# Two-layer graph attention on one core: the softmax row sums are folded to 32 partitions by transfers, and the MLP chunks run in another order

## The chip, the cores and the metric

The kernel runs on one core of one Trainium2 chip. The metric is device time in microseconds of one execution. Before the change three runs took 3472.78, 3475.09 and 3479.8 us; their median is 3475.09 us.

## What is computed

There are 16 graphs of 1024 nodes with 256 features, and an integer adjacency matrix of 1024 x 1024 for each. Two layers follow each other, each with a layer norm and a ReLU ahead of it and a residual around it. All arithmetic is float32.

```python
# layer 0, per graph: 8 heads of 32 columns, q = k = v
normed = layer_norm(h, gamma1, beta1)            # h = relu(layernorm(x))
scores = einsum('hqd,hkd->hqk', qkv, qkv) / sqrt(32)
attn   = softmax(where(adj > 0, scores, -inf))
h      = h + einsum('hqk,hkd->hqd', attn, qkv)
y      = layer_norm(h, gamma2, beta2)
x      = x + h + gelu(y @ W1 + b1) @ W2 + b2     # W1 256x1024, W2 1024x256
# layer 1, per graph: one head over all 1024 nodes
f      = relu(layernorm(x))
logits = (f@W@a_1)^T + f@W@a_2 + (f@W) @ a_12 @ (f@W)^T
a      = softmax(where(adj > 0, leaky_relu(logits, 0.2), -9e15))
x      = x + elu(f @ W_1 + (a @ f) @ W_2)
```

What matters here is the denominator of the first softmax: for each query and head, the sum over 1024 keys of the exponentials.

## The kernel before

Scores are kept transposed, with the keys on the 128 partitions and the queries along the free dimension. A **unit** of layer 0 is one block of 128 keys (`kt`, 8 of them), one half of 512 queries (`qh`, 2) and one group of 4 heads (`g`, 2), so a graph has 32 units. Units with the same `qh` and `g` form a **group** of 8. In a unit TensorE (PE) writes the scores of 4 heads (`scores`, line 990), VectorE (DVE) adds the mask out of PSUM (line 1011, two instructions of 128x1024), ScalarE (ACT) takes the exponential in place (line 1014, two instructions), and one unit later PE multiplies the values by them (`weigh`, line 1027).

The denominators are built beside that. The exponentials of `kt` 0 are written into two tiles `acc` of 128x1024 (heads 0, 1 and heads 2, 3). Those of `kt` 1 to 7 land in tiles `e`, of which there are five, and each is added to `acc` by an accumulating transfer that GpSimd (POOL) issues (`add_up`, line 1051). Each such transfer waits until the one before it on the same `acc` has landed, and an `e` tile is free again when its transfer has landed. In graph 0 the odd `kt` are added by DVE instead. After the last `kt` of a group `weigh` copies the weighed values out (`os`, line 1042) and puts the group on a list. Two units later `total` (line 924) sums `acc` over its 128 partitions: PE multiplies it by a column block of ones, four products of 512 columns, one for each head (line 929), and ACT copies the result `den` to SBUF as `ds` (line 937). `invert` (line 942) transposes `ds` by 16 small products with a selection matrix `each_head`, DVE takes the reciprocal, and `finish` transposes `os`, scales it and adds it to `h`.

Layer 0's MLP and the whole of layer 1 of graph b run while PE does the attention of graph b+1. They are a generator `rest` (line 1114), whose order is written out in lines 1341 to 1420: `expand(c)` is W1 for a chunk of 256 rows, `contract(c)` is W2 for it, then come the projections, the logits (`weights`) and the weighed sums (`attend`). Six streams (attention, rest, preparation, prologue of the next graph, masks, set-up) are merged by places in lines 1492 to 1497. A step can also be put off with `defer(us, f)`: it is issued once a running count of estimated microseconds has passed. All this only fixes the order of instructions on each engine and queue; every engine runs its own list in order, and POOL's transfers and SyncE's (SP's) transfers are each issued in list order too.

Before chunk 2 is prepared, `rest` waits (line 1348) until both groups of the second query half are finished. While it waits, attention units follow each other without MLP work between them.

Of the kernel before, what the change touches and what calls it, by code (L numbers as in the profile page):

```python
# [9 lines left out]
F32 = mybir.dt.float32  # L10
# [4 lines left out]
ALU = mybir.AluOpType  # L15

P = 128
# [477 lines left out]
def fast_path(  # L495
# [28 lines left out]
    nc = tc.nc  # L524
# [3 lines left out]
    GH = 4  # L528
# [20 lines left out]
    midp = pool("midp", 3)  # L549
    ep = pool("ep", 5)  # L550
    accp = pool("accp", 2)
    lp1 = pool("lp1", 6)
    tmpp = pool("tmpp", 2)
    smallp = pool("smallp", 3)
# [45 lines left out]

    each_head = const.tile([P, GH], F32, name="each_head")
    nc.vector.tensor_copy(each_head, ident[:, ::HD])
    ident8 = const.tile([P, P], FP8, name="ident8")
    nc.vector.tensor_copy(ident8, ident, saturate=False)
    ones = const.tile([P, HD], F32, name="ones")
# [318 lines left out]
    def total(b, qh, g, os, accs):  # L924

        den = ps_tile([P, QW], f"den_{b}_{g}_{qh}")
        for j in range(GH):
            for acc in accs:
                nc.tensor.matmul(
                    den[j * HD : (j + 1) * HD, :],  # L930
                    ones,
                    acc[j // 2][:, j % 2, :],
                    start=acc is accs[0],
                    stop=acc is accs[-1],
                )
        ds = tmpp.tile([P, QW], F32, tag="w2", bufs=3, name=f"ds_{b}_{g}_{qh}")
        nc.scalar.copy(ds, den)
        totalled.append((b, qh, g, ds, os))

    finished = {}  # L940

    def invert(b, qh, g, ds, os):

        pt = ps_tile([P, TPH, GH], f"ptds_{b}_{g}_{qh}")
        for t in range(TPH):
            for c in range(0, P, HD):
                nc.tensor.matmul(
                    pt[c : c + HD, t, :], ds[:, t * P + c : t * P + c + HD], each_head, start=True, stop=True
                )
        rl = smallp.tile([P, TPH, GH], F32, tag="rl", name=f"rl_{b}_{g}_{qh}")  # L950
        ready = defer(1.0, lambda: nc.vector.reciprocal(rl, pt))
        turns.append((1, lambda: finish(b, qh, g, rl, ready, os)))

    def finish(b, qh, g, rl, ready, os):
        h = hs[b]
        run_deferred(ready)
        finished[b, qh] = finished.get((b, qh), 0) + 1
        clock[0] += 0.5
        pt = ps_tile([P, TPH, P], f"ptos_{b}_{g}_{qh}")
        for t in range(TPH):  # L960
            nc.tensor.transpose(pt[:, t, :], os[:, t * P : (t + 1) * P], ident)
        ot = tmpp.tile([P, TPH, GH, HD], F32, tag="w2", bufs=3, name=f"ot_{b}_{g}_{qh}")
        nc.vector.tensor_mul(
            ot, pt.rearrange("p t (j d) -> p t j d", d=HD), rl.unsqueeze(3).to_broadcast([P, TPH, GH, HD])
        )
        ho = h[qh][:, :, g * P : (g + 1) * P]
        nc.gpsimd.tensor_add(ho, ho, ot.rearrange("p t j d -> p t (j d)"))

    def attention(b, st):
# [52 lines left out]
        def weigh(qh, g, kt, es):  # L1022
            if kt == 0:
                acc[g, qh] = pso.tile([P, QW], F32, tag="o", name=f"o_{b}_{g}_{qh}")
            o = acc[g, qh]
            for j in range(GH):
                nc.tensor.matmul(  # L1027
                    o[j * HD : (j + 1) * HD, :],
                    va[:, kt, (g * GH + j) * HD : (g * GH + j + 1) * HD],
                    es[j // 2][:, j % 2, :],  # L1030
                    start=(kt == 0),
                    stop=(kt == NT - 1),
                )
            if b == 0 and kt % 2:

                if kt > 1:
                    for n, (e, w) in enumerate(zip(es, odds[g, qh])):
                        defer(1.0 + 2.5 * n, lambda e=e, w=w: nc.vector.tensor_add(e, e, w))
                odds[g, qh] = es
            if kt == NT - 1:  # L1040
                c = tmpp.tile([P, QW], F32, tag="w2", bufs=3, name=f"os_{b}_{g}_{qh}")
                nc.vector.tensor_copy(c, o)
                weighed.append((b, qh, g, c, [s[g, qh] for s in (sums, odds) if s]))

        sums, odds = {}, {}


        def add_up(qh, g, kt, e, i):
            if b == 0 and kt % 2:
                return  # L1050
            nc.gpsimd.dma_start(sums[g, qh][i], e, accum_op=ALU.add)  # L1051

# [61 lines left out]
    def rest(b, st, tails):  # L1114
# [4 lines left out]
        def load(c):  # L1119
            for t in range(c * TPC, (c + 1) * TPC):  # L1120
                xt.append(xbp.tile([P, D], F32, tag="xb", name=f"xb_{b}_{t}"))
                nc.sync.dma_start(xt[t], rows(x, b, t))
# [222 lines left out]
        hid = {0: (yield from expand(0))}  # L1345
        ask(turn, 1)
        yield from tails[b]()
        while finished.get((b, 1), 0) < NG:
            yield 0.0, None
        prepare(b, st, 2)  # L1350
        load(2)
        hid[1] = yield from expand(1)
        ask(turn, 2)
        prepare(b, st, 3)
        yield from contract(0, hid[0])
        load(3)
        hid[2] = yield from expand(2)
        ask(turn, 3)
        prepare1(0)
        yield from contract(1, hid[1])  # L1360
        hid[3] = yield from expand(3)
        prepare1(1)
        fT = st["fT"] = midp.tile([P, DC, N], F32, tag="mid", name=f"fT_{b}")
# [201 lines left out]
```

## Time and profile before

| | |
|---|---|
| median of three runs | 3475.09 us |
| the profiled execution, its own time | 3465.53 us |
| its span in the trace | 3463.8 us |
| PE busy | 3421.5 us, 99% |
| DVE busy | 2751.4 us, 79% |
| ACT busy | 1857.5 us, 54% |
| POOL busy | 1416.9 us, 41% |
| accumulating transfers | 864 of 512 KB, 71.5% of the time of 16 DMA engines |
| SP's transfers | 137.56 MB, 15.9% |
| granted TensorE clock | 0.998 |

The span holds 119015 instructions. Each line of a group of instructions gives its source line, the engine, the tile written and the tiles read, the count, the busy time, the mean duration of one in nanoseconds, and the time that the engine sat idle before it with what ended that. A busy share is an average over stages with different limits. TensorE's float32 products are recorded as two passes each, so a product of the program is two records.

### The profile page before, as it was taken

The numbers are of one execution on the slowest core, as the hardware profiler recorded it, in microseconds if no ns is written. First come the engines' busy times: TensorE is split into PE (matmuls) and PEld (weight loads), VectorE is DVE, ScalarE is ACT, GpSimd is POOL, SyncE is SP. The second block draws the span as 40 slices with busy tenths as digits, with TensorE's granted clock in tenths as the row PEclk, the third lists the DMA queues.
The fourth block names the chain that finished last, engine by engine and source line by source line (L and its number), as shares of the span: only waits on it lengthen the run. The fifth ranks groups of instructions, "written<-read, shape, count | busy, mean of one in ns | idle before, by whom it ended". The sixth has DMA issues, their size and how long they took to land. (4 is left out here: it accounts for less than half of the span.)

```text
span 3463.8 us, 119015 instructions
## 1 busy us (share of the span) xinstructions
PE 3421.5 (99%) x52478; PEld 1644.7 (47%) x52478; DVE 2751.4 (79%) x5194; ACT 1857.5 (54%) x2184; POOL 1416.9 (41%) x1708
## 2 busy tenths in 40 slices
PE   7999999999999999999999999999999999999998
PEld 2344444444444444444444444444444444444477
DVE  6888788787878878888887887878878788887754
ACT  5555555555555555555555555555555555555522
POOL 4443443434444344443444434344343443433220
PEclk9999999999999999999999999999999999999999
DMA  8799989999899998999999899998999989899730
GB/s 195 154 183 181 185 164 194 177 193 185 164 185 176 185 187 169 184 171 191 189 177 186 166 189 179 188 187 168 186 178 193 186 163 184 170 193 180 153 64 14
DMA packets 281902, 598.56 MB, mean 173 GB/s; under 512 B 94880, under 2 KB 130080, under 8 KB 281376
## 3 DMA queue, kind: packets, MB, share of 16 engines
q0 software_dynamic: 124416, 453.04, 71.5%
q1 hardware_dynamic: 156672, 137.56, 15.9%
q8 instruction: 414, 6.78, 0.8%
q14 instruction: 112, 0.92, 0.1%
q10 hardware_dynamic: 288, 0.26, 0.0%
HBM read 104.21 MB, written 16.78 MB: 35 GB/s over the span
## 5 line engine op out<-in xcount | busy, mean ns | idle before, releaser
L1014 ACT ACTIVATE e<-e 128x1024 f32<-128x1024 f32 x852 | 895.9, 1057 | 947.6 <-DVE e L1011 715.3
L1051 POOL DMA_DIRECT2D acc<-e x864 | 756.2, 891 | 1447.4 <-DMA acc<-e 664.6
L1011 DVE TENSOR_TENSOR e<-s,mk 128x1024 f32<-128x1024 f32 x852 | 1004.0, 1218 | 180.1 <-PE s L990 148.4
L990 PE MATMUL s<-kT 32*64 32x512 f32 x8192 | 577.3, 615 | 2.9 <-DVE odd L1011 2.9
L1027 PE MATMUL o<-e,va 128*32 128x512 f32 x3456 | 462.9, 606 | 2.1 <-ACT e L1014 2.1
L571 PE MATMUL pa<-gw,e 128*32 128x258 f32 x7648 | 454.3, 380 | 0.6 <-issue 0.6
L571 PE MATMUL lg<-fT,uT 128*32 128x256 f32 x7680 | 448.5, 379 | 0.0
L571 PE MATMUL ph<-yT,w 128*32 128x256 f32 x7808 | 448.5, 379 | 0.0
L571 PE MATMUL po<-w,hid 128*32 128x256 f32 x7680 | 440.5, 379 | 0.0
L571 PEld LDWEIGHTS ph<-yT,w 128*32 128x32 f32 x7808 | 259.8, 110 | 197.7 <-issue 42.5
L571 PEld LDWEIGHTS po<-w,hid 128*32 128x32 f32 x7680 | 250.2, 110 | 209.1 <-issue 61.6
L571 PEld LDWEIGHTS lg<-fT,uT 128*32 128x32 f32 x7680 | 258.4, 110 | 190.1 <-issue 38.9
L571 PEld LDWEIGHTS pa<-gw,e 128*32 128x32 f32 x7648 | 249.9, 110 | 202.5 <-issue 49.9
L1287 ACT ACTIVATE e<-e,shift 128x512 f32<-128x512 f32 x256 | 183.0, 717 | 186.0 <-DVE e L1286 161.2
L1281 DVE SCALAR_TENSOR_TENSOR e<-lg,gw,mk 128x256 f32<-128x256 f32 x512 | 223.2, 478 | 71.6 <-PE lg L571 61.1
L1184 DVE TENSOR_TENSOR hid<-ph,b1c 128x512 f32<-128x512 f32 x256 | 175.6, 688 | 85.6 <-PE ph L571 74.2
L1027 PEld LDWEIGHTS o<-e,va 128*32 128x32 f32 x3456 | 68.8, 108 | 354.0 <-issue 219.9
L1286 DVE SCALAR_TENSOR_TENSOR e<-e 128x512 f32<-128x512 f32 x256 | 196.6, 768 | 8.8
L1014 ACT ACTIVATE acc<-acc 128x1024 f32<-128x1024 f32 x124 | 131.0, 1057 | 129.0 <-DVE acc L1011 124.6
L990 PEld LDWEIGHTS s<-kT 32*64 32x64 f32 x8192 | 120.6, 130 | 162.8 <-issue 105.0
L1011 DVE TENSOR_TENSOR acc<-s,mk 128x1024 f32<-128x1024 f32 x124 | 146.1, 1218 | 20.8 <-PE s L990 20.6
L815 POOL TENSOR_TENSOR nrm<-nrm,g 128x256 f32<-128x256 f32 x128 | 113.3, 885 | 60.9 <-DVE nrm L749 60.9
(146 smaller groups left out, 3817.9 us busy)
## 6 DMA issues: line engine op xcount, KB each, us to landing
acc<-e POOLq DMA_DIRECT2D x864, 512.0 KB, 6.2
adj<-in_adj_dram SPq DMA_DIRECT2D x248, 256.0 KB, 5.6
h<-in_x_dram SPq DMA_DIRECT2D x64, 256.0 KB, 6.3
xb<-in_x_dram SPq DMA_DIRECT2D x128, 128.0 KB, 4.2
out_dram<-z SPq DMA_DIRECT2D x128, 128.0 KB, 4.0
adj<-in_adj_dram SPq DMA_DIRECT2D x4, 512.0 KB, 7.1
mk<-mq SPq DMA_TRANSPOSE x128, 6.4
w<-in_L_gnn_W_dram SPq DMA_DIRECT2D x2, 1024.0 KB, 9.6
```

Source lines behind the costliest of these rows:

```text
L571: nc.tensor.matmul(out[c : c + HD], lhsT[:, c : c + HD], rhs, start=start, stop=stop)
L815: nc.gpsimd.tensor_mul(nrm, nrm, g1)
L990: nc.tensor.matmul(sc[j // 2][c : c + P // 2, j % 2, :], kT[r, g, kt * P + c : kt * P + c + P // 2], kT[r, g, qs], start=j >= by_pe, stop= ...
L1011: nc.vector.tensor_tensor(e, masked, mb, op=ALU.add)
L1014: weights = lambda e=e, masked=masked: nc.scalar.activation(e, masked, AF.Exp, scale=SCALE)
L1027: nc.tensor.matmul(o[j * HD : (j + 1) * HD, :], va[:, kt, (g * GH + j) * HD : (g * GH + j + 1) * HD], es[j // 2][:, j % 2, :], start=(kt = ...
L1051: nc.gpsimd.dma_start(sums[g, qh][i], e, accum_op=ALU.add)
L1184: nc.vector.tensor_tensor(hid[:, f0 : f0 + 2, :], ph, b1c[:, f0 : f0 + 2].unsqueeze(2).to_broadcast([P, 2, CW]), op=ALU.add,)
L1281: nc.vector.scalar_tensor_tensor(e[:, j, :], lg[:, j, :], gw[:, kt, D : D + 1], st[c // 2][:, kt // 2, qs, kt % 2], op0=ALU.add, op1=ALU.add,)
L1286: nc.vector.scalar_tensor_tensor(e, e, ALPHA, e, op0=ALU.mult, op1=ALU.max)
L1287: ready = defer(2.5, lambda: nc.scalar.activation(e, e, AF.Exp, bias=shift))
```

## The change

For graphs 1 to 14, and for the first query half of graph 15, the denominators are built in another way. That is 14 x 4 + 2 = 58 groups of 64.

- `kt` 1 is added to `acc` by two POOL instructions of 128x1024 in place of two accumulating transfers.
- After the last `kt`, `fold` issues a series of steps put off by 10, 17, 22 and 27 us of the running count. First two accumulating transfers from POOL add one half of the partitions of each `acc` to its other half (64 partitions, 256 KB each; heads 0, 1 end in partitions 0 to 63, heads 2, 3 in 64 to 127). Then eight plain transfers from SP copy quarters of 32 partitions x 512 (64 KB each) into a tile `part` of 128 x 2 x 512, so that each head has its own 32 partitions. Then one POOL instruction adds the two halves of `part` (128x512). Then the group goes to `invert`, where the 16 small products read `part` with a matrix `head_of` that sums 32 partitions.
- `total`, with its four products and its ACT copy, is left for graph 0 and for the last two groups of graph 15.
- The tag `w2` has two buffers instead of three, and `part` has one.
- In `rest`, `expand(1)` comes ahead of the wait for the second query half; after it come `contract(0)`, `contract(1)`, `expand(2)`, `expand(3)`, `contract(2)`, `contract(3)`, where it was `expand(1)`, `contract(0)`, `expand(2)`, `contract(1)`, `expand(3)`, `contract(2)`, `contract(3)`.

```diff
@@ -549,6 +549,7 @@
     midp = pool("midp", 3)
     ep = pool("ep", 5)
     accp = pool("accp", 2)
+    foldp = pool("foldp", 1)
     lp1 = pool("lp1", 6)
     tmpp = pool("tmpp", 2)
     smallp = pool("smallp", 3)
@@ -600,6 +601,10 @@
 
     each_head = const.tile([P, GH], F32, name="each_head")
     nc.vector.tensor_copy(each_head, ident[:, ::HD])
+    head_of = const.tile([P, GH], F32, name="head_of")
+    nc.gpsimd.memset(head_of, 0.0)
+    for j in range(GH):
+        nc.gpsimd.memset(head_of[j * HD : (j + 1) * HD, j : j + 1], 1.0)
     ident8 = const.tile([P, P], FP8, name="ident8")
     nc.vector.tensor_copy(ident8, ident, saturate=False)
     ones = const.tile([P, HD], F32, name="ones")
@@ -933,19 +938,45 @@
                     start=acc is accs[0],
                     stop=acc is accs[-1],
                 )
-        ds = tmpp.tile([P, QW], F32, tag="w2", bufs=3, name=f"ds_{b}_{g}_{qh}")
+        ds = tmpp.tile([P, QW], F32, tag="w2", name=f"ds_{b}_{g}_{qh}")
         nc.scalar.copy(ds, den)
-        totalled.append((b, qh, g, ds, os))
+        totalled.append((b, qh, g, ds, os, each_head))
+
+    def folds(b, qh):
+        return 0 < b and (b < B - 1 or qh == 0)
+
+    def fold(b, qh, g, os, acc):
+
+        part = foldp.tile([P, 2, QW], F32, tag="part", name=f"part_{b}_{g}_{qh}")
+        half = [slice(i * P // 2, (i + 1) * P // 2) for i in range(2)]
+        heads = [slice(j * HD, (j + 1) * HD) for j in range(GH)]
+
+        def fold_halves():
+            for i in range(2):
+                nc.gpsimd.dma_start(acc[i][half[i]], acc[i][half[1 - i]], accum_op=ALU.add)
+
+        def take_quarters():
+            for j in range(GH):
+                for i in range(2):
+                    nc.sync.dma_start(part[heads[j], i], acc[j // 2][heads[j ^ i], j % 2, :])
+
+        def join():
+            nc.gpsimd.tensor_add(part[:, 0], part[:, 0], part[:, 1])
+
+        defer(10.0, fold_halves)
+        defer(17.0, take_quarters)
+        defer(22.0, join)
+        defer(27.0, lambda: totalled.append((b, qh, g, part[:, 0], os, head_of)))
 
     finished = {}
 
-    def invert(b, qh, g, ds, os):
+    def invert(b, qh, g, ds, os, head):
 
         pt = ps_tile([P, TPH, GH], f"ptds_{b}_{g}_{qh}")
         for t in range(TPH):
             for c in range(0, P, HD):
                 nc.tensor.matmul(
-                    pt[c : c + HD, t, :], ds[:, t * P + c : t * P + c + HD], each_head, start=True, stop=True
+                    pt[c : c + HD, t, :], ds[:, t * P + c : t * P + c + HD], head, start=True, stop=True
                 )
         rl = smallp.tile([P, TPH, GH], F32, tag="rl", name=f"rl_{b}_{g}_{qh}")
         ready = defer(1.0, lambda: nc.vector.reciprocal(rl, pt))
@@ -959,7 +990,7 @@
         pt = ps_tile([P, TPH, P], f"ptos_{b}_{g}_{qh}")
         for t in range(TPH):
             nc.tensor.transpose(pt[:, t, :], os[:, t * P : (t + 1) * P], ident)
-        ot = tmpp.tile([P, TPH, GH, HD], F32, tag="w2", bufs=3, name=f"ot_{b}_{g}_{qh}")
+        ot = tmpp.tile([P, TPH, GH, HD], F32, tag="w2", name=f"ot_{b}_{g}_{qh}")
         nc.vector.tensor_mul(
             ot, pt.rearrange("p t (j d) -> p t j d", d=HD), rl.unsqueeze(3).to_broadcast([P, TPH, GH, HD])
         )
@@ -1038,15 +1069,21 @@
                         defer(1.0 + 2.5 * n, lambda e=e, w=w: nc.vector.tensor_add(e, e, w))
                 odds[g, qh] = es
             if kt == NT - 1:
-                c = tmpp.tile([P, QW], F32, tag="w2", bufs=3, name=f"os_{b}_{g}_{qh}")
+                c = tmpp.tile([P, QW], F32, tag="w2", name=f"os_{b}_{g}_{qh}")
                 nc.vector.tensor_copy(c, o)
-                weighed.append((b, qh, g, c, [s[g, qh] for s in (sums, odds) if s]))
+                if folds(b, qh):
+                    fold(b, qh, g, c, sums[g, qh])
+                else:
+                    weighed.append((b, qh, g, c, [s[g, qh] for s in (sums, odds) if s]))
 
         sums, odds = {}, {}
 
 
         def add_up(qh, g, kt, e, i):
             if b == 0 and kt % 2:
+                return
+            if kt == 1 and folds(b, qh):
+                nc.gpsimd.tensor_add(sums[g, qh][i], sums[g, qh][i], e)
                 return
             nc.gpsimd.dma_start(sums[g, qh][i], e, accum_op=ALU.add)
 
@@ -1345,19 +1382,19 @@
         hid = {0: (yield from expand(0))}
         ask(turn, 1)
         yield from tails[b]()
+        hid[1] = yield from expand(1)
         while finished.get((b, 1), 0) < NG:
             yield 0.0, None
         prepare(b, st, 2)
         load(2)
-        hid[1] = yield from expand(1)
+        yield from contract(0, hid[0])
         ask(turn, 2)
         prepare(b, st, 3)
-        yield from contract(0, hid[0])
         load(3)
+        yield from contract(1, hid[1])
+        ask(turn, 3)
         hid[2] = yield from expand(2)
-        ask(turn, 3)
         prepare1(0)
-        yield from contract(1, hid[1])
         hid[3] = yield from expand(3)
         prepare1(1)
         fT = st["fT"] = midp.tile([P, DC, N], F32, tag="mid", name=f"fT_{b}")
```

## Prediction

> **What bounds the kernel now.** I read the busy times first, then the slices, then the transfer queues.
>
> ```profile
> PE 3421.5 (99%) x52478; PEld 1644.7 (47%) x52478; DVE 2751.4 (79%) x5194; ACT 1857.5 (54%) x2184; POOL 1416.9 (41%) x1708
> PE   7999999999999999999999999999999999999998
> PEclk9999999999999999999999999999999999999999
> DMA  8799989999899998999999899998999989899730
> q0 software_dynamic: 124416, 453.04, 71.5%
> ```
>
> PE is full in every slice but the first and last, at full granted clock, so whatever leaves PE's list can shorten the run. But the transfer engines stand at 8 to 9 tenths too, most of it accumulating transfers: a second resource is nearly full. Next one graph cut into its four groups (graph 6's rest beside graph 7's attention).
>
> ```profile
> core 0: us, PE busy (x) PEld busy (x) DVE busy (x) ACT busy (x) POOL busy (x), PEclk, DMA share, GB/s
> 1411.00:1463.10 52.10, 52.10 (x856) 24.84 (x852) 38.17 (x64) 28.86 (x29) 21.55 (x27) 1.00 0.84 173
> 1463.10:1516.40 53.30, 53.30 (x851) 25.47 (x848) 47.14 (x98) 29.75 (x30) 24.69 (x32) 1.00 1.09 205
> 1516.40:1570.30 53.90, 53.90 (x821) 24.73 (x820) 42.65 (x78) 31.05 (x44) 27.11 (x33) 1.00 0.75 146
> 1570.30:1621.90 51.60, 51.60 (x854) 24.70 (x853) 46.45 (x91) 26.79 (x35) 16.85 (x20) 1.00 1.05 206
> ```
>
> PE has no gap at all: 52.7 us a group. DVE is busy 73 to 90%, and most in the last group, where the weighed sums of layer 1 run. Transfers swing around 0.93.
>
> **Part 1: the products and copies that go.** The timeline of PE around one `den`:
>
> ```profile
> 1475.77 1.07 PE L1027 MATMUL o<-e,va 128*32 128x512 f32 x8
> 1476.65 1.04 PE L929 MATMUL den<-acc,ones 128*32 128x512 f32 x8
> 1477.51 1.69 PE L571 MATMUL po<-w,hid 128*32 128x256 f32 x28
> ```
>
> The first column is the start. Ends overlap, so the price is start to start: 1477.51 - 1476.65 = 0.86 us a group. 58 x 0.86 = 49.9 us, all on the engine without gaps. ACT loses 58 copies of 0.57 us (33 us); it is at 54% and nobody waits for it there: nothing. The 16 small products of `invert` are as many and as large as before: nothing. The saving is bounded above by 49.9 us.
>
> **Part 2: POOL's additions and VectorE.** POOL loses 116 transfer issues at 0.88 us and gains as many for the halves (at most the same price). It gains 116 additions of 128x1024 and 58 of 128x512. The latter size is in the trace: shortest 1.27 us, and 128x256 takes 0.72, so 0.55 us for 256 more columns and about 2.4 us for 1024 (an estimate). That is 116 x 2.4 + 58 x 1.29 = 353 us, POOL from 1417 to 1770 us, some 52%. POOL's own load costs nothing; what it does to DVE may:
>
> ```profile
> L1286 DVE SCALAR_TENSOR_TENSOR e<-e x256: 691/692/2056, 260.0 to 3446.7; 128x512 f32<-128x512 f32 x128
> L592 DVE TENSOR_SCALAR mq<-adj x248: 362/420/2326, 53.2 to 3183.8; 128x512 fp8e5<-128x512 int32 x124
> ```
>
> Minimum, median and maximum: the long ones fall where POOL computes. In the trace such an instruction ends only some time after the POOL addition that it met, and between two POOL additions it gets through. Summed over DVE lines 1286, 592, 1333, 1334 and 749, the time above their usual durations is 54 us, beside 743 us of POOL arithmetic in some 870 instructions of about 0.85 us: 0.06 us each. The chance of meeting one and the time then lost both grow with its length, so 2.4 us costs (2.4/0.85)² x 0.06 = 0.5 us, and a group two of these and 0.15 for the last addition: 1.1 us of DVE time, 66 us in all. How much of it PE feels depends on how early DVE is done:
>
> ```profile
> 1605.70 2.36 DVE L1011 TENSOR_TENSOR e<-s,mk 128x1024 f32<-128x1024 f32 x2
> ...
> 1608.54 0.69 PE L990 MATMUL s<-kT 32*64 32x512 f32 x8
> ```
>
> DVE frees the score banks at 1608.06, PE writes the next at 1608.54: 0.5 us to spare. The units 28 to 30 of a graph are like this; the units in which the new additions fall (1, 9, 17, 25 and the ones after) have 1.8 to 3.9 us. A collision of at most 2.4 us is mostly swallowed there, and a part is handed on where DVE is at 90%. I take 12 us of the 66; bounds 0 and 66.
>
> [...]
>
> **Part 3: the chain of accumulating transfers.** This decides the sign. POOL's timeline of a group, `kt` 2's first issue, `kt` 7's two, the next group's first; the last line is from the view of the tile `acc`, least, median and most:
>
> ```profile
> 1535.75 0.89 POOL L1051 DMA_DIRECT2D acc<-e  x1 [2.62 <-DMA acc<-e]
> ...
> 1571.91 0.85 POOL L1051 DMA_DIRECT2D acc<-e  x1 [4.52 <-DMA acc<-e]
> 1574.37 0.85 POOL L1051 DMA_DIRECT2D acc<-e  x1 [1.61 <-DMA acc<-e]
> 1580.46 0.85 POOL L1051 DMA_DIRECT2D acc<-e  x1 [5.24 <-ACT e L1014]
> ...
> DMA to landing us min/median/max: 4.5/6.2/11.6
> ```
>
> From `kt` 2's first issue to `kt` 7's second landing it is 1574.37 + 6.2 - 1535.75 = 44.8 us; over the 60 groups of graphs 1 to 15 the median is 44.5 (43.5 to 46.3 for the middle eight tenths), with `kt` 1 51.8 of the 52.7 us of a group. So it runs at its own pace, 7.2 us a pair, and catches up only in `kt` 0. After the change POOL's list has the halves, which wait for `kt` 7's landing, then the two additions for `kt` 1, then `kt` 2. A group's loop is then 44.5 + 0.9 (second half's issue) + 4.8 (additions) = 50.2 us, and PE's new period is 52.7 - 0.86 = 51.9. Two things can lengthen it. The eight quarters: SP issues such loads at 0.4 to 0.6 us, so 3 to 5 us; by q1's row (137.56 MB in 15.9% of 3463.8 us) 64 KB take 0.26 us of all engines, eight 2.1. A half is half of an accumulating transfer, 2.87/2 = 1.43 us (71.5% of the span by 864 by two). Halves and quarters start in the 5.7 us in which nothing accumulates; I add 0.5 us of overlap (0 to 2.1). The last addition waits on POOL for the quarters, ahead of `kt` 3: they land about 9.5 us after `kt` 7, when POOL waits for `kt` 2 until about 12, so I add 0.5 (0 to 1.8). Sum 51.2 us, bounds 50.2 and 54.1. Against 51.9 it costs nothing while it stays below. Over the run the transfers change by -116 x 2.87 + 116 x 1.43 + 464 x 0.26 = -46 us of 16 engines.
>
> [...]
>
> **Part 4: SP's list and the MLP order.** The quarters stand in SP's list ahead of mask loads and mask transposes. SP waits there until the halves have landed, and DVE's mask conversion (line 592), which now waits 13.8 us in all for its loads, would be late by what the masks are: 0 to 3 us, twice a graph. I take 5 us for the run (0 to 90). The selected values are finished 2 to 3 units later than before; the wait in `rest` is covered by `expand(1)`, four more steps of 1.73 us on PE, and no PE unit in the changed list holds less than the 4.7 us of work that the shortest holds now. The list puts `invert` five units after the group's end, some 12 us after the last addition. The order itself removes no work: nothing. If the cover were gone, a unit with no other work is 1.93 us of PE against 2.4 of DVE and 5.7 of transfers, about 4 us of gap each, one or two a graph, 60 to 120 us.
>
> **Sum.** The profiled execution took 3465.5 us (span 3463.8 and 1.7 around it): 3465.5 - 49.9 + 12 + 0 + 5 = 3432.6. The median of the runs is 9.6 us above it: 3475.1 - 32.9 = 3442.
>
> **Rivals.** (A) The chain becomes the bound, slower than before. Place: POOL's list between `kt` 7's landing and `kt` 2's issue. It decides from a loop of 51.9 us on, and from 52.7 the run is slower. At 53.4 it gives 3475 + 58 x 0.7 = 3516. For it: it uses 98% of its group now, and transfers stand at 0.93. Against it: two accumulations of 14 leave it. (B) VectorE takes most back in the weighed-sum stage, where it is at 90% and PE gets less to do: 45 us of the 66 reach PE, giving 3475 - 50 + 45 + 5 = 3475. Against it: 1.8 to 3.9 us to spare where the additions fall. (C) The late finish or the masks open gaps of 2 us a graph: 30 us, 3475 - 50 + 12 + 30 = 3467. (D) All is hidden, 3425; it belongs to the forecast.
>
> **How the numbers follow.** Forecast with D (3425 to 3457) 0.60, A 0.20, B 0.12, C 0.08. About 0.2%, 7 us, is what a measurement can tell. Faster: 0.60, 0.07 of B, 0.03 of C: 0.70. Same: 0.03 of A, 0.04 of B, 0.03 of C: 0.10. Slower: 0.17 of A, 0.01 of B, 0.02 of C: 0.20. The range goes from the full saving, 3424, to 3500, a loop of 53.1 us; beyond it lies half of A.
>
> **What the changed profile would show.** `den` in 6 of 64 groups; PE still without gaps and the groups at 51.9 us; additions of 128x1024 near 2.4 us; longer maxima on lines 1286 and 592's successors with 60 us more in sum; `kt` 2 issued 5 to 6 us after `kt` 7's landing. I am wrong if PE shows gaps that end with DVE's mask addition, and that in turn waits for a transfer from `e` (A), or if DVE is near 100% in the last group of each graph (B).

## The result, and the profile after

The changed kernel takes 3832.2 us (median of four runs, 3823.36 to 3842.53), against 3473.94 us of the kernel before on the same chip (3467.73 to 3479.8). The ratio is 1.1033, with an interval of 1.0999 to 1.1067: slower by 358 us, where 33 us of gain were forecast.

The page of the changed kernel: busy times, slices, transfer queue, the group of the new additions and the issues of halves and quarters.

```profile
PE 3531.8 (92%) x52014; PEld 1751.3 (46%) x52014; DVE 2956.8 (77%) x5194; ACT 1833.9 (48%) x2126; POOL 1761.7 (46%) x1887
PE   7988999999989899999998989998898999989998
PEclk9999999999999999999999999999999999999999
DMA  7788878898798887878979789788897888978940
q0 software_dynamic: 116992, 422.63, 63.1%
L1086 POOL TENSOR_TENSOR acc<-acc,e 128x1024 f32<-128x1024 f32 x116 | 298.0, 2730 | 46.9 <-ACT e L1045 35.4
acc<-acc POOLq DMA_DIRECT2D x116, 256.0 KB, 5.1
part<-acc SPq DMA_DIRECT2D x464, 64.0 KB, 2.4
```

PE has lost its full slices, though it has fewer products (52014 records against 52478). No other engine has come near the top in its place: DVE is at 77%, POOL at 46%, and the accumulating transfers went from 71.5% to 63.1% of the engines' time. So nothing has become the bound by its load; PE waits somewhere. The granted clock hides in the slices' single digit, but the windows show it. These are the four groups of graph 7's attention, with PE's busy time after the length, and the granted clock behind POOL:

```profile
core 0: us, PE busy (x) PEld busy (x) DVE busy (x) ACT busy (x) POOL busy (x), PEclk, DMA share, GB/s
1571.30:1627.20 55.90, 53.73 (x855) 28.23 (x851) 36.40 (x61) 28.47 (x28) 26.06 (x28) 0.97 0.83 167
1627.20:1682.10 54.90, 54.52 (x838) 28.79 (x837) 48.76 (x99) 29.26 (x29) 29.94 (x34) 1.00 0.87 183
1682.10:1743.10 61.00, 55.96 (x809) 25.00 (x808) 49.34 (x80) 30.44 (x43) 35.27 (x39) 0.94 0.70 138
1743.10:1807.00 63.90, 54.64 (x842) 26.76 (x841) 51.60 (x89) 26.32 (x34) 21.66 (x21) 0.95 0.89 163
```

The loss is not even: 3.8 and 1.6 us in the first two groups, 7.1 in the third, 12.3 in the fourth. In the third the transfers stand at 0.70 (0.75 before). Cut finer, by the start of each unit's score products (means over graphs 2 to 13, in us; the gaps are PE's own above 0.1 us, in brackets; "late invert" is an experiment told below that has the new order of PE's list and none of the fold's work):

| units of a graph | before | late invert | changed |
|---|---|---|---|
| 6 and 7 | 12.7 | 16.8 | 20.1 (2.0) |
| 11 to 13 | 20.3 | 20.4 (0.2) | 24.5 (2.3) |
| 18 | 8.7 | 8.7 | 13.3 (5.0) |
| 19 | 6.4 | 5.5 | 7.2 |
| 26 and 27 | 13.6 | 12.7 | 14.0 (0.7) |
| 29 | 6.5 (0.1) | 8.4 (0.8) | 16.9 (7.3) |
| a whole graph | 211.3 (0.2) | 213.3 (1.5) | 236.7 (18.1) |

Two places, units 18 and 29, hold more than half of it. Besides, with every gap of 4 us or more in graphs 1 to 14 the granted clock falls to 0.5, during the gap or within half a microsecond after it, and stays there for 3.4 to 13.7 us. Summed as (1 - granted) x duration over the execution that is 127 us, against 8 before; 39 of the 127 lie inside the gaps. In units 18 and 19 a gap of 5.0 us costs 7.1 in all: they last 20.4 us, and 13.3 in the run told below in which that gap is gone. The order of PE's list moves work from unit to unit, so the changed kernel is to be read against the second column.

**Unit 18.** The timeline of the changed kernel, start and duration, three engines:

```profile
1697.16 5.86 DVE L748 TENSOR_SCALAR ve_b<-mv_b 128x2 f32<-128x2 f32 x1
1697.73 5.25 POOL L1086 TENSOR_TENSOR acc<-acc,e 128x1024 f32<-128x1024 f32 x2
1702.94 2.34 DVE L1042 TENSOR_TENSOR e<-s,mk 128x1024 f32<-128x1024 f32 x2
1706.21 1.08 PE L828 MATMUL ptk<-ident,va 128*128 128x128 f32 x4 [5.01 <-DVE e L1318]
```

An instruction of two columns, 0.17 us elsewhere, stands on DVE from before the first new addition until the second one ends. The mask additions behind it in DVE's list are late, and so is the instruction of layer 1 (line 1318) behind these, for which PE waits 5.01 us.

**Unit 29.** The same view, four engines:

```profile
1764.22 9.12 SPq L961 DMA_DIRECT2D part<-acc  x8
1776.46 1.28 POOL L964 TENSOR_TENSOR part<-part 128x512 f32<-128x512 f32 x1 [6.49 <-DMA part<-acc]
1777.68 1.80 POOL L1088 DMA_DIRECT2D acc<-e  x2
1777.71 5.49 SPq L907 DMA_TRANSPOSE mk<-mq  x2
1789.64 0.86 POOL L1088 DMA_DIRECT2D acc<-e  x1 [10.16 <-DMA acc<-e]
1789.22 1.22 DVE L1042 TENSOR_TENSOR e<-s,mk 128x1024 f32<-128x1024 f32 x1 [6.01 <-DMA acc<-e]
1790.67 1.93 PE L572 MATMUL pf<-wo,fT 128*32 128x256 f32 x16 [8.85 <-DVE dens L1361]
```

SP takes 9.1 us to issue the eight quarters. POOL waits 6.5 us for them in the last addition, so the next accumulating transfers are issued at 1777.7, at the moment when SP issues two mask transposes; the transfers land only about 11 us later, where 6.0 us is the median of the run. DVE then waits 6 us for an `e` tile, and PE 8.9 us for DVE. Whether the transposes slow the transfers beside them was not tried by itself.

### The profile page after: what moved, and what is told of

Its sections match the earlier page's. It is cut to its first block, busy times and chain, and to the rows that moved or that the text cites. A ratio compares the mean times of both kernels' runs of the same rounds, so it can differ in the third digit from the quotient of the medians.

```text
span 3840.8 us, 119489 instructions
## 1 busy us (share of the span) xinstructions
PE 3531.8 (92%) x52014; PEld 1751.3 (46%) x52014; DVE 2956.8 (77%) x5194; ACT 1833.9 (48%) x2126; POOL 1761.7 (46%) x1887
## 3 DMA queue, kind: packets, MB, share of 16 engines
q0 software_dynamic: 116992, 422.63, 63.1%
## 5 line engine op out<-in xcount | busy, mean ns | idle before, releaser
L1088 POOL DMA_DIRECT2D acc<-e x748 | 657.3, 909 | 1240.0 <-DMA acc<-e 630.1
L1021 PE MATMUL s<-kT 32*64 32x512 f32 x8192 | 668.4, 637 | 28.8 <-DVE e L1042 24.5
L1058 PE MATMUL o<-e,va 128*32 128x512 f32 x3456 | 483.4, 622 | 2.2 <-ACT e L1045 2.1
L572 PE MATMUL po<-w,hid 128*32 128x256 f32 x7680 | 449.9, 386 | 24.7 <-ACT hid L1228 24.5
L572 PEld LDWEIGHTS po<-w,hid 128*32 128x32 f32 x7680 | 310.1, 112 | 180.5 <-issue 50.7
L572 PEld LDWEIGHTS lg<-fT,uT 128*32 128x32 f32 x7680 | 271.7, 110 | 188.8 <-issue 54.9
L1086 POOL TENSOR_TENSOR acc<-acc,e 128x1024 f32<-128x1024 f32 x116 | 298.0, 2730 | 46.9 <-ACT e L1045 35.4
L1021 PEld LDWEIGHTS s<-kT 32*64 32x64 f32 x8192 | 137.8, 134 | 252.7 <-DVE e L1042 105.8
L1323 DVE SCALAR_TENSOR_TENSOR e<-e 128x512 f32<-128x512 f32 x256 | 241.8, 945 | 8.8
L572 PE MATMUL pf<-wo,fT 128*32 128x256 f32 x1920 | 137.3, 405 | 103.7 <-DVE dens L1361 103.5
L593 DVE TENSOR_SCALAR mq<-adj 128x512 fp8e5<-128x512 int32 x248 | 182.1, 766 | 40.2 <-DMA adj<-in_adj_dram 39.9
```

What stands on the lines that cost most here:

```text
L572: nc.tensor.matmul(out[c : c + HD], lhsT[:, c : c + HD], rhs, start=start, stop=stop)
L593: nc.vector.tensor_scalar(m[:, i * QW : (i + 1) * QW], a, 0.0, NEG8, op0=ALU.is_le, op1=ALU.mult, saturate=False)
L1021: nc.tensor.matmul(sc[j // 2][c : c + P // 2, j % 2, :], kT[r, g, kt * P + c : kt * P + c + P // 2], kT[r, g, qs], start=j >= by_pe, stop= ...
L1058: nc.tensor.matmul(o[j * HD : (j + 1) * HD, :], va[:, kt, (g * GH + j) * HD : (g * GH + j + 1) * HD], es[j // 2][:, j % 2, :], start=(kt = ...
L1086: nc.gpsimd.tensor_add(sums[g, qh][i], sums[g, qh][i], e)
L1323: nc.vector.scalar_tensor_tensor(e, e, ALPHA, e, op0=ALU.mult, op1=ALU.max)
```

## The experiments

All are compared with runs of the kernel before on the same chip; differences below are against those.

### First round: one part undone, or one part alone

**kt 1 by accumulating transfers again**, all else as changed:

```diff
-            if kt == 1 and folds(b, qh):
-                nc.gpsimd.tensor_add(sums[g, qh][i], sums[g, qh][i], e)
-                return
             nc.gpsimd.dma_start(sums[g, qh][i], e, accum_op=ALU.add)
```

> The changed kernel with kt 1 added by two accumulating transfers again, the rest of the fold kept. Theory 1 (the chain of accumulating transfers, lengthened by the fold's waits on POOL, sets the pace): a pair costs 7.2 us in place of two additions of 2.65 each, so the loop grows by about 2 us a group; 3830 to 3950 us, with DVE's mask addition waiting longer for transfers from e. Theory 2 (VectorE is blocked through both POOL additions): the 5 us gap in unit 18 of each graph goes, with the slow clock after it, 68 + 50 us or so: 3700 to 3730 us. Theory 3 (the order of the MLP chunks): 3832 us, unchanged.

3778.95 us, ratio 1.0879 (1.085 to 1.0908). The gap of unit 18 is gone (7.8 us where it was 13.3), but the run wins only 55 us: units 6, 12 and 20 to 22, which now have a transfer more in the chain, hold new gaps, and unit 29 keeps 4.6 us.

**The order of the MLP chunks alone**, in the kernel before:

> The kernel before with only the MLP chunks in the new order. Theory 3: much of the loss is there already, 3600 us or more. Theories 1 and 2: 3474 us within 10, since neither the transfers nor POOL's work is touched.

3491.56 us, ratio 1.0047 (1.0029 to 1.0066): 16 us lost. **The old order in the changed kernel:**

> The changed kernel with the MLP chunks in the old order. Theories 1 and 2: the gaps of units 13, 18 and 29 stay (37 + 68 + 105 us); the gap of unit 7 may go or grow, as the wait for the second query half stands open a unit earlier: 3800 to 3900 us. Theory 3: near 3430 us.

3924.82 us, ratio 1.1281 (1.1256 to 1.1306), 91 us slower than the changed kernel. Units 3 to 5 then last 3.8, 2.6 and 3.5 us, with no MLP work to cover the wait for the finish, and what was held back follows in units of 10 to 18 us. So the new order costs a little and is needed once the finish is late.

**kt 1 by POOL additions alone**, in the kernel before:

> The kernel before with kt 1 added by POOL in the same 58 groups; no fold, den by PE as before. Theory 2: the gaps of unit 18 appear here too, 68 us and the slow clock after them: 3540 to 3600 us. Theory 1: the chain gets one pair shorter and nothing waits in POOL's list; 3465 to 3480 us.

3540.85 us, ratio 1.0184 (1.0165 to 1.0202): 65 us lost. Its timeline beside unit 18:

```profile
1563.65 4.71 POOL L1052 TENSOR_TENSOR acc<-acc,e 128x1024 f32<-128x1024 f32 x2
1564.21 1.84 DVE L743 TENSOR_SCALAR ve_b<-mv_b 128x2 f32<-128x2 f32 x1
1565.96 2.34 DVE L1011 TENSOR_TENSOR e<-s,mk 128x1024 f32<-128x1024 f32 x2
```

Here DVE gets through between the two additions: the same small instruction ends at 1566.0, when the first addition has ended, and the mask additions then run at their usual speed beside the second one. In unit 18 DVE is thus held up by about one addition here and by two in the changed kernel. Ahead of unit 10 of this run both additions hold it: two instructions of 128x256 (line 749, 0.41 us elsewhere) take 2.47 and 2.46 us, one beside each. PE's own waits end elsewhere than in the changed kernel:

```profile
PE ph L571 <- ACT ds L937: 22.3, 14, 1.7
PE puT L571 <- ACT ds L937: 18.9, 13, 1.5
```

The columns are the sum in us, the number of waits and the longest one. The late mask additions make ACT late, and with it the copy `ds` of `den`, which PE waits for. The changed kernel has no such copy in these groups, so the 65 us are not a part of its loss as they stand.

**A gap between the two additions**, on top of that run; the copy reads what the first addition wrote:

```diff
+                if i:
+                    gap = smallp.tile([P, 1], F32, tag="gap", name=f"gap_{b}_{g}_{qh}")
+                    nc.gpsimd.tensor_copy(gap, s[0][:, 1, QW - 1 : QW])
                 nc.gpsimd.tensor_add(s[i], s[i], e)
```

> The kernel before with kt 1 on GpSimd (3541), and one GpSimd copy of 128x1 between the two additions, which reads the first one's output and so can't start before it has ended. T2 in its strict form, VectorE is locked out because the second addition starts without a gap: tiny VectorE instructions no longer stand for 5 us at unit 18, its 21 us gap goes, 3475 to 3510. If the length of the additions alone counts, or the changed distance of the transfers: 3530 to 3560.

3534.73 us, ratio 1.0185 (1.0166 to 1.0205), the same as without the gap: the median distance of the two additions grew from about 0 to 0.2 us and nothing followed. So the missing distance between the two is not what costs there. Whether such a gap would free DVE in the changed kernel, where it was held through both, was not tried.

### Second round: the wait of the last addition

The first round left the fold itself as the largest part, and POOL's wait for the quarters as the suspect. **The two partial sums added by PE** (32 small products in the place of 16), so that POOL waits for no quarter:

```diff
-        defer(22.0, join)
-        defer(27.0, lambda: totalled.append((b, qh, g, part[:, 0], os, head_of)))
+        defer(27.0, lambda: totalled.append((b, qh, g, part, os, head_of)))
...
+                parts = [ds] if head is each_head else [ds[:, 0], ds[:, 1]]
+                for n, d in enumerate(parts):
+                    nc.tensor.matmul(
+                        pt[c : c + HD, t, :],
+                        d[:, t * P + c : t * P + c + HD],
+                        head,
+                        start=n == 0,
+                        stop=n == len(parts) - 1,
+                    )
```

> The changed kernel without GpSimd's addition of the two partial sums: invert adds them in PSUM, by 32 small products in the place of 16, so nothing on GpSimd waits for the quarters any more. PE gets 58 x 16 more small products; at some 0.02 to 0.03 us each that is 20 to 27 us. T1, the chain of accumulating transfers is held up by the addition that waits for the quarters: the gaps of units 29, 7 and 13 (166 us of the 269, and their share of the lost clock) go, unit 18 stays: 3560 to 3650. T2, VectorE's long stops behind two GpSimd additions in a row are the main cause: about 3810 to 3850. T4, the slow issue of the quarters and of the mask loads and transposes behind them in SP's list, or the halves' own wait, is what holds the chain: the gaps of unit 29 stay, 3750 to 3850.

3808.65 us, ratio 1.0964 (1.0933 to 1.0995): a gain of 20 us, where the suspicion asked for 180. The 32 products take 0.79 us a group where 16 took 0.46, some 19 us over the run, so without them the gain would be near 39 us. Units 6 and 7 became clean (16.8 us, as with the late invert), but unit 29 kept its gap of 7.5 us. Its waits:

```profile
POOL acc L1090 <- DMA acc<-e: 572.3, 262, 8.8
DVE mq L593 <- DMA adj<-in_adj_dram: 148.3, 50, 8.0
PE pf L572 <- DVE dens L1363: 90.0, 14, 8.0
```

DVE's wait for mask loads, 13.8 us before and 39.9 in the changed kernel, is 148 now: a second wait had stood behind the first, and took its place. **The last addition put later**, behind `kt` 4's transfers:

```diff
-        defer(22.0, join)
-        defer(27.0, lambda: totalled.append((b, qh, g, part[:, 0], os, head_of)))
+        defer(32.0, join)
+        defer(37.0, lambda: totalled.append((b, qh, g, part[:, 0], os, head_of)))
```

> The changed kernel with the last addition put ten cost units later in the list, and invert too, so that GpSimd comes to it behind kt 4's accumulating transfers, when the quarters have long landed. T1: like the run with that addition on PE, 3540 to 3650, since only the wait mattered. If it is the addition itself, or the transfers of halves and quarters: 3780 to 3850.

3834.8 us, ratio 1.1036 (1.1008 to 1.1064): no gain; the wait for mask loads is 125 us, and the finish came so late that units 6 and 7 of the next graph had no MLP work. **Both at once, the sums on PE and kt 1 by transfer:**

> As e5, and kt 1's weights added by accumulating transfers again, so that both suspected costs on GpSimd are gone: no addition of 128x1024 and none that waits for quarters. What is left of the change are the halves, the quarters, 32 small products in the place of den, and the order of the MLP chunks. T1 with T2: the chain holds seven pairs and the halves, 52 to 54 us a group against PE's 52.3, so 3440 to 3530. T4: the gaps of units 29 and 6 stay as in the run with kt 1 by transfer (3779): 3700 to 3790.

3735.62 us, ratio 1.0791 (1.0744 to 1.0838). Neither of the two suspects is left in this kernel and still 265 us are lost: the theory that POOL's waits and additions explain most of the loss has fallen.

### Third round: where the quarters are issued

All of these start from the kernel with both suspects removed.

**Quarters ten cost units later in SP's list:**

```diff
-        defer(17.0, take_quarters)
-        defer(27.0, lambda: totalled.append((b, qh, g, part, os, head_of)))
+        defer(27.0, take_quarters)
+        defer(37.0, lambda: totalled.append((b, qh, g, part, os, head_of)))
```

> As the run with the sums added on PE and kt 1 by transfer (3736), with the quarters ten cost units later in SP's list, and invert too. SP then reaches them when the halves have long landed. T4a, SP's wait for the halves (764 us in all in that run) holds back the mask loads and transposes behind it: that wait shrinks to under 200 us, VectorE's waits for mask loads in line 593 fall from 92 us to the 14 of the kernel before, 3500 to 3600. T4b, the issuing itself is too slow (eight quarters in 9.5 us): 3680 to 3760.

3750.31 us, ratio 1.0804 (1.0775 to 1.0833). The total lies in the range of the second theory (T4b), but the units show that it came about in another way: unit 29 fell from 15.0 us (gap 5.3) to 7.3 (gap 0.1), and the wait for mask loads from 92 to 29 us; but the later finish left units 5 to 7 of the next graph with 24 to 56 records of PE in place of 124 to 152, and units 9 and 10 grew from 5.5 and 7.2 us to 19.5 and 12.9. What one won, the other lost. SP's wait for the halves fell only from 764 to 568 us.

**Quarters issued from ACT's queue**, put off by 22 and `invert` by 32:

```diff
-                    nc.sync.dma_start(part[heads[j], i], acc[j // 2][heads[j ^ i], j % 2, :])
+                    nc.scalar.dma_start(part[heads[j], i], acc[j // 2][heads[j ^ i], j % 2, :])
```

> As the run with the sums added on PE and kt 1 by transfer (3736), with the quarters issued from ScalarE's queue, five cost units later so that ScalarE seldom waits for the halves; SP's list is that of the kernel before. T4 (SP's list, whether by wait or by issue): VectorE's waits for mask loads fall to some 14 us and the gap of unit 29 goes: 3480 to 3580, if eight issues of up to 1.2 us on ScalarE don't hold up the exponentials. If the transfers of halves and quarters themselves crowd the accumulations (T5): 3650 to 3760, with POOL waiting for DMA as before.

3868.61 us, ratio 1.1113 (1.1066 to 1.116), worse: ACT stood idle for 214 us ahead of exponentials until transfers of the quarters had landed, and PE waited 192 us for those exponentials. Unit 29 did fall, from 15.0 to 11.0 us. So the wait was moved into a list that PE depends on more; the run doesn't clear SP.

**No quarters**, the head sums taken from the halves by 64 small products; **and no halves either**, 64 products straight from the 128 partitions of `acc` (`ds` is `acc` in these lines):

```diff
+                for j in range(GH):
+                    nc.tensor.matmul(
+                        pt[c : c + HD, t, j : j + 1],
+                        ds[j // 2][:, j % 2, t * P + c : t * P + c + HD],
+                        head[:, j // 2 : j // 2 + 1],
+                        start=True,
+                        stop=True,
+                    )
```

> As the run with the sums added on PE and kt 1 by transfer (3736), without the quarters: invert takes the sums of each head straight from the halves, by 64 small products in the place of 32. PE gets 58 x 32 small products more, some 0.4 us a group, 25 us. T4 or T5 by the quarters: 3500 to 3580. If the halves on GpSimd's queue hold the chain: 3680 to 3780.

> As the run without quarters, and without the halves too: 64 small products take the sums straight from the 128 partitions of acc; no den, no copy, kt 1 by transfer, the new order of the MLP chunks. The transfers are those of the kernel before. PE has 0.86 us a group less of den and some 0.85 us more of small products, so it should stand beside the new order alone (3492): 3470 to 3520 if the fold's transfers are all that is wrong. If late sums, held tiles or the small products cost more than that: above 3550.

3688.46 us, ratio 1.0608 (1.0577 to 1.0638), and 3651.81 us, ratio 1.0522 (1.0482 to 1.0562). The first differs from the second by the halves and stands 37 us above it. The second has the transfers of the kernel before and yet loses 182 us. These two were bad instruments: the 64 small products take 2.69 us a group where 16 took 0.46, which with `den` gone is 58 x (2.69 - 0.46 - 0.86) = 79 us more, and (1 - granted) x duration sums to 87 us, as the last section tells. With the 22 us of the next experiment that is about the whole.

### Fourth round: one cause at a time, added to the kernel before

**The late invert alone.** New order, `den` as before, and `invert` put off so that it stands in units 5, 13, 21 and 29, as in the changed kernel:

```diff
-        totalled.append((b, qh, g, ds, os))
+        if folds(b, qh):
+            defer(14.0, lambda: totalled.append((b, qh, g, ds, os)))
+        else:
+            totalled.append((b, qh, g, ds, os))
```

> The kernel before with the new order of the MLP chunks (3492), where den is computed as before, but invert is listed 14 cost units later, so that it and the transposes after it stand in the units of a graph in which the changed kernel has them (5, 13, 21, 29 in the place of 3, 11, 19, 27). No transfer is added or taken away. If the late place of invert is a main cause, as the run without any fold (3652) would have it: 3560 to 3660, gaps at units 6, 7 and 13. If that run was slow because of its 64 small products alone: 3480 to 3520.

3492.99 us, ratio 1.006 (1.0041 to 1.0079): 22 us, 6 more than the order alone, and the two intervals overlap. The late place is nearly harmless as long as it is no later.

**The quarters added to that**, in the place in SP's list that they have in the changed kernel, and used by nothing (`quarters_of` makes `part` and puts `take_quarters` off by 17 us, as `fold` does):

```diff
                 nc.vector.tensor_copy(c, o)
+                if folds(b, qh):
+                    quarters_of(b, qh, g, sums[g, qh])
```

> As the late invert alone, and in each of the 58 groups SP also issues the eight quarters where the changed kernel has them; nothing uses what they bring. The difference to the late invert alone is the price of the quarters in SP's list and on the transfer engines. T4, that they hold back the mask loads and transposes: a gap of 4 to 7 us at unit 29 in each graph, 90 to 180 us more. If the quarters are harmless by themselves: within 25 us.

3639.52 us, ratio 1.0485 (1.046 to 1.051): 147 us more. SP and DVE near unit 29 without the quarters, and then with them:

```profile
1600.31 1.97 SPq L902 DMA_TRANSPOSE mk<-mq  x1
1606.83 0.82 SPq L584 DMA_DIRECT2D adj<-in_adj_dram  x2
1615.30 0.75 DVE L592 TENSOR_SCALAR mq<-adj 128x512 fp8e5<-128x512 int32 x2
```

```profile
1657.94 10.78 SPq L954 DMA_DIRECT2D part<-acc  x8
1668.76 2.34 SPq L903 DMA_TRANSPOSE mk<-mq  x1
1671.20 2.59 SPq L585 DMA_DIRECT2D adj<-in_adj_dram  x2
1679.02 0.88 DVE L593 TENSOR_SCALAR mq<-adj 128x512 fp8e5<-128x512 int32 x2 [6.01 <-DMA adj<-in_adj_dram]
1683.67 1.94 PE L572 MATMUL pf<-wo,fT 128*32 128x256 f32 x16 [6.62 <-DVE dens L1344]
```

This is the mechanism in five lines. SP would have issued the transpose at about 1658; now the eight quarters are ahead of it for 10.8 us. The mask load behind the transpose goes out at 1671.2 and has landed by 1679.0, DVE stands at the conversion for 6 us, and the mask addition of the next scores stands behind the conversion, as does what PE waits for, 6.6 us. Unit 29 takes 15.2 us in place of 8.4. In units 5 and 21 the same quarters cost nothing; in units 12 and 13, where masks are turned too, 2.4 us. This run also has two buffers for the tag `w2` in place of three, as the changed kernel has. The run without one set of quarters, told below, has them too and stands 21 us above the late invert, so they hold no more than that.

**The halves added to the late invert**, with `den` taken from them by the same eight products (weights zero in the other half), two units later:

```diff
+                defer(10.0, fold_halves)
+                defer(17.0, lambda: weighed.append((b, qh, g, os, [acc])))
...
-                    ones,
+                    half_of[:, j // 2, :] if folds(b, qh) else ones,
```

> As the late invert alone, with the halves on GpSimd's queue as in the changed kernel, and den taken from the halves by the same eight products with weights that are zero in the other half, two units later than in the kernel before. No quarters, no addition on GpSimd. The difference to the late invert alone is the price of the halves. If they fit in the time in which nothing accumulates, as the prediction had it: within 25 us. If they hold up the chain: 50 to 150 us more, with gaps of VectorE's mask addition that end with acc<-e.

3554.62 us, ratio 1.0222 (1.0178 to 1.0266): 62 us more. POOL's wait for landing transfers rose from 631 to 812 us. But most of the lost time (3.2 us a graph after the 0.86 that moved in) is in unit 28, where PE waits for ACT's copy of the `den` that was moved there. The changed kernel has no such copy there. So 62 us is more than the halves cost in this arrangement; on the base of the 64 small products it was 37.

**The fold in one group of four alone**, the second one of the first half, old order, kt 1 by transfer:

> The kernel before with the fold in one group of four alone (second group of the first half, where the other runs lost least), kt 1 by transfer, the old order of the MLP chunks. It takes 15 x 0.86 = 13 us from PE. If a fold costs nothing where its invert stands away from the mask loads and the MLP's start: 3460 to 3470, faster than before. If it pays the 4 us a group that units 19 to 22 lost in the run with kt 1 by transfer: 3500 to 3530.

3531.2 us, ratio 1.0184 (1.0149 to 1.0218): even there a fold costs some 4 us a graph, with gaps of 1.2, 0.5 and 0.9 us in units 20 to 22. No version was found that beats the kernel before.

**The quarters of one group left out** of the idle quarters, the first group of the second half, whose quarters stand beside unit 29; and **the fold left out in that group** of the changed kernel:

```diff
-                if folds(b, qh):
+                if folds(b, qh) and (qh, g) != (1, 0):
```

In the changed kernel kt 1's addition has the same condition, so that group's kt 1 goes by transfer.

> The run with idle quarters (3640), without the quarters of that one group; the other three of each graph have theirs. If the price of the quarters is the mask loads that stand behind them in SP's list at unit 29: 3493 to 3520, as the late invert alone or little above. If each set of quarters costs its share: 3600.

> The changed kernel without the fold in one group of each graph, the first of the second half (units 16 to 23), whose second accumulation on GpSimd stands beside unit 18 and whose quarters stand beside unit 29; that group keeps den and its transfers as before. If the losses are local, as the units of the changed kernel and of the idle quarters show: units 16 to 31 fall from 124 us to some 108 a graph, 14 x 16 = 225 us less, 3580 to 3640. If they come from the fold's total load, a quarter of the 357 us goes: 3730 to 3760.

3517.72 us, ratio 1.0111 (1.0081 to 1.0142): one set of quarters in four was 126 of the 147 us, and three sets with the two buffers of `w2` the other 21. And 3651.88 us, ratio 1.0485 (1.0446 to 1.0524): 181 of the 358 us go with that one group, where an even share (14 of 58 groups) would be 86. It is less than the 225 expected, because its neighbours got slower: units 20 to 22 and 26 hold 3.0 us of gaps that they had not. Unit 29 is back at 6.5 us and unit 18 at 7.8.

## Why the prediction was wrong

**Part 1 was right.** Unit 2 goes from 7.25 to 6.39 us, the 0.86 us of `den`, and units 10, 18 and 26 lose as much in the runs in which they have no new gap: 49.9 us in all. It was a gain of PE's work, and the waits took it back.

**Part 2: the length of an addition was right, what it costs was not.** An addition takes 2.37 us in the median in the run with kt 1 alone, as estimated (2.4), and 2.73 us in the mean in the changed kernel. The term "1.1 us of DVE time, 66 us in all" was too small: DVE is busy 103 us longer in the run with kt 1 alone (2854.4 against 2751.4) and 205 us longer in the changed kernel (2956.8). The step that failed with it is that DVE gets through "between two POOL additions" and that a collision "is mostly swallowed there", 12 us. Alone the additions cost 65 us, five times that, though PE's waits are others there; taken out of the changed kernel they give back 55, and without them units 18 and 19 are 7.1 us a graph shorter. The spare time of a unit was set against one collision drawn by chance. The list makes it the same one in every graph: in unit 18 two additions hold one instruction for 5.9 us, and both mask additions stand behind it. In the run with kt 1 alone the small instruction of unit 18 ends 0.02 us after the first addition; in the changed kernel it is held through a second one. The 65 and 55 us of the runs lie near the prediction's upper bound of 66, far from the 12 that it took.

**Part 3: the loop was the wrong place to look.** The chain did not become the bound as a loop of POOL's list: taking the join's wait off POOL, the term that was given 0.5 us a group (bounds 0 to 1.8), gave 20 us in all, or 39 without the added products of that run. The wait itself was mis-sized:

```profile
POOL part L964 <- DMA part<-acc: 172.1, 32, 7.8
```

That is 5.4 us each in 32 of the 58 groups. The sign that was named, `kt` 2 issued 5 to 6 us after `kt` 7's landing, came out at 12.0 us in the median (with 6.0 us to land); how much of it only follows from PE's own delays was not separated. The halves cost 37 or at most 62 us where they were tried.

**Part 4 is the step that failed most.** "[DVE's mask conversion] would be late by what the masks are: 0 to 3 us, twice a graph. I take 5 us for the run (0 to 90)." The quarters alone cost 147 us. Three things were too small in it. Their issue was put at 3 to 5 us: the median of one is 0.59 us, but beside the mask work eight took 9.1 and 10.8 us. The load's lateness on SP was then taken as DVE's lateness up to 3 us, while SP's order put a transpose between quarters and load as well, and DVE's wait was 6.0 us. And the price of PE's wait was taken without the clock, which was 0.5 for 6.8 us or more at unit 29 in 13 of 14 graphs with the idle quarters and in 12 of 14 in the changed kernel.

**What no term held.** The parts, each by its own run, sum to

| part | us |
|---|---|
| order and late invert | +22 |
| quarters in SP's list | +147 |
| halves, with the moved `den` | +62 |
| kt 1 on POOL | +65 |
| den gone, Part 1 | -50 |
| sum | +246 |
| measured | +358 |

The 112 us between are what the parts do to each other, and the table is no account of single causes: 44 us of PE's gaps with kt 1 alone and 34 with the halves end with ACT's copy `ds`, which the changed kernel lacks in these groups. Unit by unit, the late invert and the differences of the three parts, without the 0.86 us of `den`, can be set beside the changed kernel. They fall short of it by 5.4 us a graph in units 18 and 19, where two additions hold DVE for 5.9 us in place of 1.8; by 3.3 in units 6 and 7; by 2.1 in units 26 and 27; by 2.4 in unit 29. They are too high by 3.2 in unit 28 and by 2.8 in units 10, 15 and 16. Units 6 and 7 lose their 3.3 us only with the join on POOL (16.8 us again without it), some 47 us over the run. Which pair makes the rest, the runs do not say.

Of the rivals, A had the sign and the place of the wait (a gap of PE that ends with DVE, and that with a transfer from `e`), but at 3516 it held a ninth of the loss. C, the late masks, had the mechanism that proved largest, at 2 us a graph where it is 10 (147 us over 15 graphs). Neither price held anything for the clock.

## What to carry to other kernels

When a change puts transfers into a queue, list what stands behind them in that queue and ask when each of those is needed, unit by unit; a mean slack over the period says nothing, since here three of four sets were nearly free and the fourth cost 126 us. When one wait is taken away and the time stays, look for the wait that took its place in the same unit. To size causes that cover each other, add them singly to the good kernel rather than take them singly from the bad one: the single removals of the first two rounds gave 55, 20 and -6 us, while the additions gave 147, 62 and 65. Then see in each such run whether its wait is one of the bad kernel's: two of these three held waits for a copy that the bad kernel doesn't make.

## What the runs showed of the hardware

**After many tiny products in a row the granted clock fell to 0.50, though PE shows no gap.** In the run without any fold, three windows and PE's timeline, at unit 5 of graph 7:

```profile
1510.50:1516.00 5.50, 5.50 (x176) 4.00 (x176) 3.31 (x4) 2.11 (x2) 1.44 (x2) 1.00 0.88 185
1516.00:1519.40 3.40, 3.40 (x29) 1.80 (x28) 1.26 (x2) 0.00 (x0) 0.00 (x0) 0.50 1.06 227
1519.40:1528.00 8.60, 8.60 (x160) 4.39 (x147) 4.73 (x11) 6.46 (x5) 4.60 (x5) 1.00 0.85 188
```

```profile
1512.46 2.59 PE L962 MATMUL ptds<-half_of,acc 128*32 128x1 f32 x125
1515.01 2.68 PE L571 MATMUL ph<-yT,w 128*32 128x256 f32 x29
```

PE is busy for the whole of all three windows, and about 0.9 us after 2.6 us of products with one column the clock falls to 0.50 for 3.4 us. The run has 40 such stretches, 87 us of lost clock, against 5 us in the run with the order alone and 16 with the late invert, which has 32 records of four columns in the same units. 37 of the 40 lie in units 5, 13, 21 and 29, where these products stand, and before 31 of them PE shows no gap over 0.05 us for 8 us. So half speed followed stretches which the profile shows as fully busy; in the changed kernel, where it comes with every gap of 4 us or more in graphs 1 to 14, it lasts 3.4, 6.8, 10.2 or 13.7 us beside these gaps. What brings the clock down, and what sets these lengths, was not tried.

**The time to issue a quarter was not constant.** One of 64 KB took SP 0.51 us at least, 0.59 in the median and 2.09 at most in the changed kernel, 370 us for all 464. In the run with the sums on PE and kt 1 by transfer, eight in a row beside the mask work took 9.53 us. What sets it was not tried.

**A small DVE instruction was held through two GpSimd additions** (5.86 us against 0.17) in the changed kernel, and through one (1.84 us) in the run with kt 1 alone. In both the second addition starts before the record of the first one ends, by 0.62 and by 0.04 us. What makes the difference stays open.
